# Gated cross-attention stack on one core: the first batch's loads come first, other preparation is queued behind its steps, and a sigmoid is written with tanh

## The chip, the core and the metric

The kernel runs on one core of one Trainium2 chip. The core has five engines that work side by side, each through its own queue in order: TensorE (PE: matmuls and transposes into PSUM banks), VectorE (DVE), ScalarE (ACT), GpSimd (POOL) and SyncE (SP, which here issues nearly all DMA loads and stores). The metric is the device time of one execution in microseconds (us), as the median of the runs shown.

## The reference

The input `x` has 8 batches of 256 tokens with 256 features, and the context `ctx_1024` the same shape. Four gated blocks follow one another:

```python
x = x + tanh(g_xattn[0]) * L0_xattn(layernorm(x), ctx)           # 16 heads of 16, keys and values from ctx
x = x + tanh(g_ffn[0])   * L0_slots(layernorm(x))                # routes to 64 slots, top 8, GRU update, gather back
x = x + tanh(g_xattn[1]) * L1_xattn(ctx, layernorm(x))           # 8 heads of 128 over 512 keys (ctx and x)
x = x + tanh(g_ffn[1])   * L1_ffn(layernorm(x), clip_x, clip_down)   # int8 fake-quantized gated FFN
```

The last block scales its activations by `sigmoid(clip) * max(abs(.)) / 127`, with one `clip` for its input and one for its hidden layer. The maximum of the input is taken over all batches, so that block starts when all the others are done.

## The kernel before

All tokens stay on the chip: `xs[b]` and `cs[b]` hold batch b of `x` and of the context, 128 partitions by 2 x 256. Layer 0 runs batch by batch. Batches 0 and 1 take a way of their own at the start; batches 2 to 7 are fed piece by piece into layer 1's loop from a queue (`side`). Layer 1's attention loops over 8 batches and 8 heads and takes most of the time; the FFN comes last.

**Tile framework.** The code records instructions; a scheduler then fixes the order of each engine's queue and inserts semaphore waits. So the order in the code is only a preference, unless there is a dependency. `tc.issue_after(ins)` puts what is recorded inside it behind `ins` where both are on the same engine. It adds no waiting on another engine.

**One batch of layer 0** (`Batch0`), in steps: `norm` (statistics and normalization on DVE, the power -1/2 on POOL: `ln_stats` L231, `ln_apply` L243), `turn_c` and `turn_x` (transposes on PE, copied out by ACT and DVE), `key` and `query` (projection L506 on PE, bias on ACT L528 and L520, then `split` L471, which splits the result into a high and a low part on DVE), `stack` (for batches 0 and 1 `spread` L550: small matmuls that place each head's rows into the operands `ks` and `qs`, copied out half by DVE L565 and half by ACT L566), `scores` (matmul L598, maximum on DVE L601), `maxima` (transposes L611, copied by ACT L612 into `qs`), `exps` (matmul L622, exponential on ACT L625), `sums`, `divide`, and at the end `turn_o` and `finish` (output projection L671 and residual add L678). Each batch has four groups of four heads. The operands carry eight more rows for the maxima; those of `ks` are filled once with the constant `pick` (DVE L192, four operands). Batch 0 uses the `m` banks of PSUM, batch 1 and later ones the `z` banks.

**Weights.** `wk` and `wq` exist in two layouts: as loaded (`wk_n`, `wq_n`, used by batches 0 and 1), and reordered by ACT (`by_place`, L174) for batches 2 to 7.

**Fill.** The slot block's weights must be transposed first: `fill` is a list of twelve pieces (`turn_slots`, `turn_w1`, `bias1`, three turns each for `wih` and `whh`, `gh`, `wv`, `wo`). A turn is four PE transposes (L254) into the one `s` bank and an ACT copy (L322). They are staged in memory that layer 1's weights take over later.

**The order at the start.** The SP queue issues the loads in code order: the context of batch 0, Wk, x of batch 0, Wq, two biases, Wv, bv, batch 1, Wo, then scalars, three bias rows broadcast to 128 partitions, the slot weights and the rest. Loads share eight semaphores in turn, so that each load waits for the one eight places before it. Constants are filled by POOL and DVE as they are allocated. Then batch 0 and batch 1 are interleaved by this loop:

```python
HEAD, LAG = 5, 10
for _, go in work0[0][:HEAD]:
    go()                          # norm, turn_c, key, turn_x, query of batch 0
second.pop(0)()                   # norm of batch 1
gates()
for n, go in enumerate(first):    # the rest of batch 0
    go()
    if n < len(fill):
        fill[n]()
    if n >= LAG:
        second.pop(0)()
by_place()
```

`gates` computes the tanh gates, the sigmoid of the two clips and the scalar `tau` on ACT, and scales three bias rows on POOL. After the loop come layer 1's loads, the first slot set (batch 0) and the rest of batch 1. Layer 1's first step, `media`, normalizes the context of batch 0.

Of the kernel before, what the change touches and what calls it, by code (L numbers as in the profile page):

```python
# [9 lines left out]
F32 = mybir.dt.float32  # L10
# [3 lines left out]
AF = mybir.ActivationFunctionType  # L14
ALU = mybir.AluOpType
# [4 lines left out]
P = 128  # L20
B, S, D = 8, 256, 256
EPS = 1e-5
H0, DK0 = 16, 16
HG = 4
NG = H0 // HG
NROW = 4 * DK0
# [63 lines left out]
def flamingo_kernel(ctx: ExitStack, tc: tile.TileContext, a: dict, out: bass.AP):  # L90
    nc = tc.nc
    V, A, G, T = nc.vector, nc.scalar, nc.gpsimd, nc.tensor
# [14 lines left out]
    x_in = a["x"].rearrange("b (t p) d -> b p t d", p=P)  # L107
    c_in = a["ctx_1024"].rearrange("b (t p) d -> b p t d", p=P)
    xs, cs = [], []
# [4 lines left out]
    def load_tokens(b, queue):  # L114
        queue.dma_start(out=xs[b], in_=x_in[b])
        queue.dma_start(out=cs[b], in_=c_in[b])
# [37 lines left out]
    wk, wq = (w0.tile([P, 2, D], F32, tag=n, name=n) for n in ("wk", "wq"))  # L154
    bk_n, bq_n = (pp_.tile([P, 2], F32, tag=n, name=n) for n in ("bkn", "bqn"))
    bk, bq = (w0.tile([P, 2], F32, tag=n, name=n) for n in ("bk", "bq"))
    nc.sync.dma_start(out=cs[0], in_=c_in[0])
    nc.sync.dma_start(out=wk_n, in_=a["L0_xattn_Wk"].rearrange("(c p) n -> p c n", p=P))
    nc.sync.dma_start(out=xs[0], in_=x_in[0])
    nc.sync.dma_start(out=wq_n, in_=a["L0_xattn_Wq"].rearrange("(c p) n -> p c n", p=P))  # L160
    for t, name in ((bk_n, "L0_xattn_bk"), (bq_n, "L0_xattn_bq")):
        nc.sync.dma_start(out=t, in_=a[name].rearrange("(c p) -> p c", p=P))
    wv = weight(w0, "wv", a["L0_xattn_Wv"], D)
    bv = rows(w0, "bv", a["L0_xattn_bv"], D, nc.sync)
    load_tokens(1, nc.sync)
    wo = weight(w0, "wo", a["L0_xattn_Wo"], D)

    def load_by_place():
# [5 lines left out]
    def by_place():  # L174
        for t, n in ((wk, wk_n), (wq, wq_n)):
            A.copy(t.rearrange("p c (e h) -> p c e h", e=DK0), n.rearrange("p c (h e) -> p c e h", e=DK0))
        G.tensor_scalar(bq4, bq, DK0**-0.5, None, ALU.mult)
# [5 lines left out]
    pick = w0.tile([2 * HG, HG], F32, tag="pick", name="pick")  # L183
    V.tensor_tensor(pick, ident[: 2 * HG, :HG], ident[: 2 * HG, HG : 2 * HG], ALU.add)

    def operand_pairs(pool, n):

        pairs = []
        for i in range(n):
            q = pool.tile([NROW + 2 * HG, HG, S], F32R, tag=f"qs{i}", name=f"qs{i}")  # L190
            k = pool.tile([NROW + 2 * HG, HG, S], F32R, tag=f"ks{i}", name=f"ks{i}")
            V.tensor_copy(k[NROW:, :, :], pick[:, :, None].to_broadcast([2 * HG, HG, S]))  # L192
            pairs.append((q, k))
        return pairs


    pairs_a, pairs_b = operand_pairs(pp_, 2), operand_pairs(w0, 2)

# [4 lines left out]
    for which, width, first, second in (("q", 160, 2, 3), ("k", 144, 1, 3)):  # L205
        t = pp_.tile([P, 4, width], F32R, tag=f"spread{which}", name=f"spread{which}")
# [6 lines left out]
    ident_b = keep.tile([P, P], BF16, tag="identb", name="ident_b")  # L213
    V.tensor_copy(ident_b, ident)
    ones = keep.tile([P, P], F32, tag="ones", name="ones")
    G.memset(ones, 1.0)
    mhalf = keep.tile([P, 2], F32, tag="mhalf", name="mhalf")
    G.memset(mhalf, -0.5)

# [22 lines left out]

    def ln_apply(dst, src, mv, scale):  # L243
        for i in range(2):
            V.tensor_scalar(
                dst[:, i, 0:D], src[:, i, :], mv[:, i, 0:1], scale[:, i : i + 1], ALU.subtract, ALU.mult
            )

    def transpose_pair(src, tag):

# [6 lines left out]
    def add_bias(b, row):  # L257
        return [G.tensor_tensor(xs[b][:, t, :], xs[b][:, t, :], row, ALU.add) for t in range(2)][-1]
# [14 lines left out]

    def gates():
        A.activation(gate, scal[:, 0:4], AF.Tanh)
        A.activation(clip, scal[:, 5:7], AF.Sigmoid)
        A.activation(tau, scal[:, 4:5], AF.Abs)
        V.tensor_scalar(tau, tau, 0.1, None, ALU.add)
        V.reciprocal(itau, tau)
        for row, g in ((gbo_a, g_x0), (gbo_f, g_f0), (gbo_b, g_x1)):  # L280
            G.tensor_scalar(row, row, g, None, ALU.mult)
# [148 lines left out]

    bq4 = w0.tile([P, 2], F32, tag="bq4", name="bq4")
    bq4_n = pp_.tile([P, 2], F32, tag="bq4n", name="bq4n")
    G.tensor_scalar(bq4_n, bq_n, DK0**-0.5, None, ALU.mult)

    def values_tile(pool):
        v = pool.tile([P, 2, H0, 2 * DK0], F32, tag="ve", name="ve")
        G.memset(v[:, :, :, DK0:], 1.0)
        return v

    places = {"a": (pp_, pairs_a, values_tile(pp_)), "b": (at0, pairs_b, values_tile(w0))}  # L440
    xn1 = w0.tile([P, 4, D + 1], F32, tag="xn1", name="xn1")
    G.memset(xn1[:, :, D : D + 1], 1.0)

    class Batch0:

# [25 lines left out]
        def split(self, name, full):  # L471

            hi, lo = self.halves(name)
            V.tensor_copy(hi, full)
            eng = V if self.b < 2 else G
            eng.tensor_tensor(lo, full, hi.bitcast(F32), ALU.subtract)
            if self.b < 2:
                return hi, lo
            name += self.s
            d = dram.tile([2, D, S], F32, tag=f"d{name}", name=f"d{name}")  # L480
            for i, x in enumerate((hi, lo)):
                nc.sync.dma_start(out=d[i].rearrange("(m p) t -> p m t", p=P), in_=x.bitcast(F32))
            return d.rearrange("i (e h) t -> i e h t", e=DK0)

        def norm(self):
            b = self.b
            self.xn = self.tmp(name="xn")
            mv, rstd = ln_stats(xs[b], "a" + self.s)
            ln_apply(self.xn, xs[b], mv, rstd)
            if b > 1:  # L490
                add_bias(b, gbo_a)

# [8 lines left out]
        def project(self, w, src):  # L501

            pp = self.bank().rearrange("p (m t) -> p m t", m=2)
            for m in range(2):
                for c in range(2):
                    T.matmul(  # L506
                        pp[:, m, :],
                        w[:, c, m * P : (m + 1) * P],
                        src[:, c, :],
                        start=c == 0,  # L510
                        stop=c == 1,
                    )
            return pp

        def query(self):
            w, bias = (wq_n, bq4_n) if self.b < 2 else (wq, bq4)
            pp = self.project(w, self.xnT)
            q = self.tmp(name="q")
            for m in range(2):
                A.activation(q[:, m, :], pp[:, m, :], AF.Identity, bias=bias[:, m : m + 1], scale=DK0**-0.5)  # L520
            self.dq = self.split("q", q)

        def key(self):
# [64 lines left out]
        def scores(self, g, qc):  # L588

            q, k = self.pairs[g % 2]  # L590
            if qc == 0:
                self.nm[g] = small.tile([P, 2, 2 * HG], F32R, tag=f"nm0{self.s}", name="nm0")
            full = small.tile([P, HG], F32, tag=f"nf0{self.s}", name="nf0")
            for half in range(2):
                ps = self.bank().rearrange("p (h k) -> p h k", h=2)
                for i in range(2):
                    j = 2 * half + i
                    T.matmul(  # L598
                        ps[:, i, :], q[:NROW, j, qc * P : (qc + 1) * P], k[:NROW, j, :], start=True, stop=True
                    )  # L600
                V.tensor_reduce(full[:, 2 * half : 2 * half + 2], ps, AX.X, ALU.max, negate=True)  # L601
            hi = self.nm[g][:, qc, :HG]
            V.tensor_copy(hi, full)
            V.tensor_tensor(self.nm[g][:, qc, HG:], full, hi.bitcast(F32), ALU.subtract)

        def maxima(self, g):

# [6 lines left out]
        def exps(self, g, half):  # L614

            q, k = self.pairs[g % 2]
            e = self.pool.tile([P, 2, 2, S], F32, tag="e", name="e", bufs=2)
            for i in range(2):
                j = 2 * half + i
                ps = self.bank().rearrange("p (c t) -> p c t", c=2)  # L620
                for kc in range(2):
                    T.matmul(  # L622
                        ps[:, kc, :], k[:, j, kc * P : (kc + 1) * P], q[:, j, :], start=True, stop=True
                    )
                A.activation(e[:, i, :, :], ps, AF.Exp)  # L625
            self.e[half] = e

        def sums(self, g):
# [309 lines left out]
    load_tokens(2, nc.sync)  # L938
    for c in range(2):
        nc.sync.dma_start(out=w1kv[:, c, :INNER], in_=a["L1_xattn_Wkv"][c * P : (c + 1) * P, :INNER])  # L940
    HEAD, LAG = 5, 10
    for _, go in work0[0][:HEAD]:
        go()
    first = [go for _, go in work0[0][HEAD:]]
    second = [go for _, go in work0[1]]
    second.pop(0)()
    gates()
    for b in range(2):
        add_bias(b, gbo_a)
    for n, go in enumerate(first):  # L950
        go()
        if n < len(fill):
            fill[n]()
        if n >= LAG:
            second.pop(0)()
    by_place()
    load_layer1()
    for _, go in slot_sets[0].pieces():
        go()
# [285 lines left out]
    def attention1():  # L1245
# [8 lines left out]
            return steps[n] if n < len(steps) else None  # L1254

        first = bs[0]
        first.media()
        first.latents()
        first.turn("m")
        first.turn("l")  # L1260
# [251 lines left out]
```

## Time and profile before

| | before |
|---|---|
| median of 3 runs | 1047.76 us (1046.73 to 1048.28) |
| profiled execution | 1043.28 us |
| its span in the profile | 1041.5 us |
| busy: PE, DVE, ACT, POOL | 990.5, 623.7, 463.9, 121.5 us |
| mean granted clock of PE | 0.975 |

The span runs from the first to the last instruction in the trace; 1.8 us of the execution lie around it. The granted clock is the share of PE's full clock that the chip's throttle let through, by stretch. Matmuls are pipelined and their ends are modelled, so a PE that is shown busy can still be slow or partly waiting. In the prediction's lines, the timeline gives start and length in us, engine, line, operation, output and input tiles, and in brackets the idle time of the engine before it with what ended it.

### The profile page before, as it was taken

To read this page: it belongs to the slowest core of one execution; us is meant where nothing else is said; L and a number is where in the kernel's file an instruction comes from. 1 tells how busy PE (TensorE), PEld (TensorE's weight loads), DVE (VectorE), ACT (ScalarE), POOL (GpSimd) and SP (SyncE) were. 2 spreads that over 40 slices of the span, in tenths; PEclk is the share of its full clock that TensorE was granted. 3 is DMA by queue.
4 is the path that set the end of the run, shared out by engine and by line. 5 is a ranking of instruction groups with operands and counts; after the bars stand their busy time and mean duration, and the time that the engine had idled before them with its cause. 6 is when DMAs were issued, how large, how long until landed. Compare 5 with 4: busy or idle time off the path is not lost.

```text
span 1041.5 us, 13065 instructions
## 1 busy us (share of the span) xinstructions
PE 990.5 (95%) x4803; PEld 683.5 (66%) x4803; DVE 623.7 (60%) x1613; ACT 463.9 (45%) x878; POOL 121.5 (12%) x158
## 2 busy tenths in 40 slices
PE   5998799999999999999999999999999999999776
PEld 4765466667677667777776676676776776776423
DVE  5655566656465655756566564566765365454397
ACT  3666335444435533444534434444334234234474
POOL 5201120101010010111001000010000000000134
PEclk9989889999999999999999999999999999999897
DMA  7702200021110101111000100001000000000002
GB/s 172 200 1 72 91 21 21 28 74 41 52 50 22 51 31 41 36 46 41 21 21 31 51 21 21 29 1 56 1 1 1 1 0 1 1 1 1 1 0 82
DMA packets 33536, 37.32 MB, mean 36 GB/s; under 512 B 10368, under 2 KB 28992, under 8 KB 33472
## 3 DMA queue, kind: packets, MB, share of 16 engines
q1 hardware_dynamic: 33472, 36.48, 11.9%
q8 instruction: 38, 0.62, 0.2%
q14 instruction: 26, 0.21, 0.1%
HBM read 28.08 MB, written 8.39 MB: 35 GB/s over the span
## 4 chain that ended last, share of the span: by engine, by line
PE 87%; DVE 7%; ACT 2%; DMA 2%; issue 1%; POOL 1%; SPq 0%; DVEq 0%; ACTq 0%; POOLq 0%
PE bank_m L1020 11%; PE bank_m L1051 11%; PE bank_m L1079 10%; PE bank_m L1033 10%; PE bank_m L1005 6%; PE bank_m L1065 5%; PE bank_m L1092 5%; PE bank_z L598 4%; PE bank_z L635 3%; PE bank_z L622 3%; PE bank_z L506 2%; PE bank_z L535 1%; PE bank_s L845 1%; PE bank_z L671 1%; PE bank_m L254 1%; PE bank_m L635 1%
## 5 line engine op out<-in xcount | busy, mean ns | idle before, releaser
L1053 ACT ACTIVATE e<-bank_m,nm 128x512 f32<-128x512 f32 x128 | 88.0, 688 | 146.2 <-DVE nm L1052 144.0
L1051 PE MATMUL bank_m<-k,q 128*128 128x512 f32 x256 | 127.3, 602 | 0.0
L1020 PE MATMUL bank_m<-kvT,w1kv 128*128 128x512 f32 x256 | 126.1, 604 | 0.0
L1079 PE MATMUL bank_m<-eT,v 128*128 128x256 f32 x512 | 124.8, 381 | 1.1 <-ACT e L1053 0.7
L1079 PEld LDWEIGHTS bank_m<-eT,v 128*128 128x128 f32 x512 | 95.3, 190 | 34.4 <-issue 16.3
L1033 PE MATMUL bank_m<-w1kv,kvT 128*128 128x256 f32 x512 | 116.6, 380 | 0.0
L1052 DVE TENSOR_REDUCE nm<-bank_m 128x1 f32<-128x512 f32 x128 | 87.9, 688 | 33.7 <-PE bank_m L1051 32.9
L1033 PEld LDWEIGHTS bank_m<-w1kv,kvT 128*128 128x128 f32 x512 | 95.9, 190 | 13.7 <-issue 1.1
L625 ACT ACTIVATE e<-bank_z 128x512 f32<-128x512 f32 x112 | 63.2, 596 | 80.9 <-PE bank_z L622 80.7
L240 POOL TENSOR_TENSOR rstd<-rstd,mhalf 128x2 f32<-128x2 f32 x48 | 34.7, 726 | 446.6 <-DVE rstd L239 410.1
L1014 DVE TENSOR_SCALAR q<-bank_m,bq 128x256 f32<-128x256 f32 x64 | 28.1, 479 | 97.1 <-PE bank_m L1005 97.0
L601 DVE TENSOR_REDUCE nf<-bank_z 128x2 f32<-128x512 f32 x112 | 75.0, 683 | 18.0 <-PE bank_z L598 17.6
L1040 DVE COPY v<-bank_m 128x512 f32<-128x512 f32 x64 | 43.9, 686 | 58.0 <-PE bank_m L1033 58.0
L1065 PEld LDWEIGHTS bank_m<-ident,e 128*128 128x128 f32 x512 | 58.5, 140 | 23.4 <-issue 18.2
L1065 PE MATMUL bank_m<-ident,e 128*128 128x128 f32 x512 | 71.4, 275 | 0.4 <-DVE v L1040 0.4
L1022 ACT ACTIVATE k<-bank_m,bk 128x512 f32<-128x512 f32 x64 | 44.0, 688 | 55.2 <-PE bank_m L1020 55.1
L1086 ACT ACTIVATE oT<-bank_m,bv 128x256 f32<-128x256 f32 x64 | 30.3, 474 | 84.4 <-PE bank_m L1079 84.1
L1005 PE MATMUL bank_m<-kvT,w1q 128*128 128x256 f32 x256 | 64.1, 388 | 1.3 <-DVE kvT L991 1.0
L1055 DVE TENSOR_SCALAR e<-e,rs 128x512 f32<-128x512 f32 x128 | 62.1, 485 | 2.2
L1051 PEld LDWEIGHTS bank_m<-k,q 128*128 128x128 f32 x256 | 44.5, 190 | 26.6 <-issue 22.0
L1020 PEld LDWEIGHTS bank_m<-kvT,w1kv 128*128 128x128 f32 x256 | 43.0, 190 | 28.1 <-issue 24.6
L1092 PE MATMUL bank_m<-w1o,oT 128*128 128x256 f32 x256 | 59.6, 380 | 0.6 <-DVE x L1106 0.6
(345 smaller groups left out, 1547.8 us busy)
## 6 DMA issues: line engine op xcount, KB each, us to landing
qs<-dqb SPq DMA_DIRECT2D x96, 64.0 KB, 2.5
ks<-dkb SPq DMA_DIRECT2D x48, 128.0 KB, 2.7
c<-in_ctx_dram SPq DMA_DIRECT2D x8, 256.0 KB, 3.2
x<-in_x_dram SPq DMA_DIRECT2D x8, 256.0 KB, 2.9
w1kv<-in_L_xattn_Wkv_dram SPq DMA_DIRECT2D x4, 512.0 KB, 6.8
out_dram<-y SPq DMA_DIRECT2D x8, 256.0 KB, 2.1
dqb<-hi SPq DMA_DIRECT2D x6, 256.0 KB, 2.1
dqb<-lo SPq DMA_DIRECT2D x6, 256.0 KB, 2.4
```

What stands on the lines that cost most here:

```text
L601: V.tensor_reduce(full[:, 2 * half : 2 * half + 2], ps, AX.X, ALU.max, negate=True)
L625: A.activation(e[:, i, :, :], ps, AF.Exp)
L1005: T.matmul(pq[:, i, :], w1q[:, c, h * P : (h + 1) * P], self.kvT[:, c, S:], start=c == 0, stop=c == 1,)
L1020: T.matmul(pk, w1kv[:, c, h * P : (h + 1) * P], self.kvT[:, c, :], start=c == 0, stop=c == 1)
L1033: T.matmul(pv[:, k, :], self.kvT[:, c, kc * P : (kc + 1) * P], w1kv[:, c, at : at + 2 * P], start=c == 0, stop=c == 1,)
L1051: T.matmul(ps, self.q[h][:, qc * P : (qc + 1) * P], self.k[h], start=True, stop=True)
L1052: V.tensor_reduce(nm[:, at], ps, AX.X, ALU.max, negate=True)
L1053: A.activation(e[:, qc, :], ps, AF.Exp, bias=nm[:, at], accum_out=sums[:, at])
L1055: V.tensor_scalar(e[:, qc, :], e[:, qc, :], rs[:, at], None, ALU.mult)
L1065: T.transpose(pt[:, k, qc * P : (qc + 1) * P], self.e[h][:, qc, kc * P : (kc + 1) * P], ident)
L1079: T.matmul(po, self.v[h // 2][:, kc, (h % 2) * P : (h % 2 + 1) * P], self.eT[:, kc, :], start=kc == 0, stop=kc == 3,)
L1092: T.matmul(self.pp[:, qc, :], self.oT[:, h, qc * P : (qc + 1) * P], w1o[:, h, :], start=h == 0, stop=h == H1 - 1,)
```

## The change

Five things change together.

1. **Loads.** SP issues x and the context of batch 0, then Wk, Wq, then batch 1, then Wv, bv and Wo. The two biases are issued by ACT's queue.
2. **Constants.** The fills of the maxima rows of the second batch's two `ks` operands (`rows_for_maxima(pairs_b)`), of `ve`, `ones` and `xn1`, and the scaling of the query bias, stand behind steps of the first batch: POOL's behind its first power, DVE's behind the key split of batch 0.
3. **Sigmoid.** `sigmoid(c)` becomes `0.5 * tanh(0.5 * c) + 0.5`: the ACT function is Tanh, as for the gates, and DVE does one more small operation. `gates` stands behind batch 0's query bias on ACT.
4. **Second batch and fill.** The pieces of batch 1 start two places earlier in the loop (LAG 8), but behind batch 0's query projection on PE and its query split on DVE. The fill starts seven places later (FILL).
5. **Reordered weights and layer 1.** `by_place` moves into the loop, behind the first exponentials of batch 0 on ACT. Layer 1's first `media` stands behind the last maxima of batch 0 on DVE.

```diff
-    nc.sync.dma_start(out=cs[0], in_=c_in[0])
+    load_tokens(0, nc.sync)
     nc.sync.dma_start(out=wk_n, in_=a["L0_xattn_Wk"].rearrange("(c p) n -> p c n", p=P))
-    nc.sync.dma_start(out=xs[0], in_=x_in[0])
     nc.sync.dma_start(out=wq_n, in_=a["L0_xattn_Wq"].rearrange("(c p) n -> p c n", p=P))
     for t, name in ((bk_n, "L0_xattn_bk"), (bq_n, "L0_xattn_bq")):
-        nc.sync.dma_start(out=t, in_=a[name].rearrange("(c p) -> p c", p=P))
+        nc.scalar.dma_start(out=t, in_=a[name].rearrange("(c p) -> p c", p=P))
+    load_tokens(1, nc.sync)
     wv = weight(w0, "wv", a["L0_xattn_Wv"], D)
     bv = rows(w0, "bv", a["L0_xattn_bv"], D, nc.sync)
-    load_tokens(1, nc.sync)
...
-            V.tensor_copy(k[NROW:, :, :], pick[:, :, None].to_broadcast([2 * HG, HG, S]))
...
+    def rows_for_maxima(pairs):
+        for _, k in pairs:
+            V.tensor_copy(k[NROW:, :, :], pick[:, :, None].to_broadcast([2 * HG, HG, S]))
+
+    rows_for_maxima(pairs_a)
...
-        A.activation(clip, scal[:, 5:7], AF.Sigmoid)
+        A.activation(clip, scal[:, 5:7], AF.Tanh, scale=0.5)
         A.activation(tau, scal[:, 4:5], AF.Abs)
+        V.tensor_scalar(clip, clip, 0.5, 0.5, ALU.mult, ALU.add)
...
+    def fill_constants():
+        G.tensor_scalar(bq4_n, bq_n, DK0**-0.5, None, ALU.mult)
+        for _, _, v in places.values():
+            G.memset(v[:, :, :, DK0:], 1.0)
+        G.memset(ones, 1.0)
+        G.memset(xn1[:, :, D : D + 1], 1.0)
...
-    HEAD, LAG = 5, 10
-    for _, go in work0[0][:HEAD]:
-        go()
-    first = [go for _, go in work0[0][HEAD:]]
-    second = [go for _, go in work0[1]]
-    second.pop(0)()
-    gates()
+    def after(*instructions):
+        stack = ExitStack()
+        for ins in instructions:
+            stack.enter_context(tc.issue_after(ins))
+        return stack
+
+    b0 = batches0[0]
+    first, second = ([go for _, go in work0[b]] for b in range(2))
+    first.pop(0)()
+    with after(b0.normed, powers[0]):
+        fill_constants()
+    HEAD, LAG, FILL = 4, 8, 7
+    for _ in range(HEAD):
+        first.pop(0)()
+    with after(b0.split_ins):
+        rows_for_maxima(pairs_b)
+        second.pop(0)()
+    with after(b0.bias_ins):
+        gates()
     for b in range(2):
         add_bias(b, gbo_a)
+    query_ins, split_ins = b0.project_ins, b0.split_ins
     for n, go in enumerate(first):
         go()
-        if n < len(fill):
-            fill[n]()
+        if n >= FILL and n - FILL < len(fill):
+            with after(query_ins):
+                fill[n - FILL]()
         if n >= LAG:
-            second.pop(0)()
-    by_place()
+            with after(query_ins, split_ins):
+                second.pop(0)()
+        if n == LAG:
+            with after(b0.exp_ins):
+                by_place()
...
-        first.media()
+        with tc.issue_after(batches0[0].max_ins):
+            first.media()
```

`normed`, `split_ins`, `project_ins`, `bias_ins`, `max_ins` and `exp_ins` are new names for the last instruction of the step in question. Lines of the changed kernel are some 10 to 30 higher: L613 is the score reduction (L601 before), L822 the first transpose of the routing weights in the slot block (L810 before).

## The prediction

> **What bounds the kernel now.** Three views, from coarse to fine: the slices of the page, busy time by stretch, and the timeline and waits of the first 30 us. The times are those of the one profiled execution.
>
> ```profile
> PE   5998799999999999999999999999999999999776
> PEclk9989889999999999999999999999999999999897
> DMA  7702200021110101111000100001000000000002
> ```
>
> TensorE (PE) is full from the second slice (26 us each) to the last three. A gain must remove PE idle time or time at a slow clock; it lies in the first four slices. In the next view, by stretch, the first pair of numbers is the stretch and its length, PEclk the granted clock.
>
> ```profile
> 0.00:10.00 10.00, 1.09 (x4) 0.72 (x4) 4.73 (x15) 3.87 (x4) 6.10 (x24) 1.00 0.67 192
> 10.00:20.00 10.00, 6.37 (x21) 5.20 (x22) 6.98 (x22) 3.11 (x7) 6.69 (x8) 0.88 0.77 115
> 60.00:65.00 5.00, 4.61 (x26) 3.15 (x24) 3.22 (x9) 4.67 (x9) 0.00 (x0) 1.00 0.00 0
> 65.00:70.00 5.00, 5.00 (x18) 2.49 (x18) 3.26 (x9) 1.31 (x3) 0.00 (x0) 0.54 0.00 0
> 70.00:75.00 5.00, 5.00 (x37) 3.42 (x36) 1.19 (x7) 1.83 (x2) 0.00 (x0) 0.77 0.00 0
> 90.00:95.00 5.00, 3.50 (x33) 2.33 (x25) 2.93 (x11) 4.07 (x8) 3.31 (x4) 1.00 0.49 125
> ```
>
> PE idles 12.5 us in the first 20, then almost nothing until 60. A hold at 60 to 62.6 is followed by a stretch at 0.54 and 0.77 of the clock, worth 5 x 0.46 + 5 x 0.23 = 3.45 us. At 90 to 95 it idles 1.5 us. The timeline shows what the first batch waits for (start, length, idle before it):
>
> ```profile
> 7.54 0.28 POOL L433 TENSOR_SCALAR bq4n<-bqn 128x2 f32<-128x2 f32 x1 [3.33 <-DMA bqn<-in_L_xattn_bq_dram]
> 7.74 3.30 DVE L192 CAST ks<-pick 8x1024 fp32r<-8x1024 f32 x4
> 9.30 2.28 POOL L240 TENSOR_TENSOR rstd<-rstd,mhalf 128x2 f32<-128x2 f32 x2
> 11.07 0.74 DVE L245 TENSOR_SCALAR x<-x,mv,rstd 128x256 f32<-128x256 f32 x2
> 11.37 0.69 PE L254 MATMUL bank_z<-ident,c 128*128 128x128 f32 x2 [6.65 <-DMA c<-in_ctx_dram]
> 15.82 1.28 ACT L276 ACT_TABLE_LOAD   x1
> 18.86 2.99 PE L506 MATMUL bank_m<-c,c 128*128 128x256 f32 x8
> 19.62 0.82 DVE L346 TENSOR_SCALAR slots<-slots,sscale 128x256 f32<-128x256 f32 x1 [1.60 <-DMA sscale<-in_L_ffn_slot_scale_dram]
> 27.13 1.29 DVE L601 TENSOR_REDUCE nf<-bank_m 128x2 f32<-128x512 f32 x2 [0.27 <-PE bank_m L598]
> ```
>
> The first batch's rstd waits behind a bias load and fills on POOL, its normalization behind four fills on VectorE (DVE). Its key projection waits behind the second batch's transposes on PE, its query projection (18.86) behind the second batch's key projection, whose input waits for the table load on ScalarE (ACT). The slots row matters most below.
>
> **Loads, POOL and ACT at the start.** With x0, c0, Wk, Wq first in the SP queue, the four land as the first four did: used at 3.52, 4.27, 6.36 and 7.09. The two bias loads go to the ACT queue beside them; their own landing took 4.2 to 4.5 us, so x0 lies between 3.5 and 4.5. I take 3.5: it decides nothing. The statistics end at 4.7, POOL's power takes 0.7, two fills instead of four 1.65, so x0 is normalized near 7 and not 11.8. ACT loses both weight copies here (2 x 1.05). The key projection runs from 6.4, as Wk lands, to 9.5; transposes and copy add 1.2; the query projection takes 10.7 to 13.7 (3.0 as in its row) instead of 18.86 to 21.85. So far the first batch leads by 8 us.
>
> **Where that lead goes.** In the built order, the slots multiply stands on DVE right behind the first batch's key split, ahead of the first ks copy and of the query split. It waits for four loads on SP, each of which also waits for the load eight places earlier. The same bytes stand ahead of them, the three 128 KB bias rows among them; while these run, 13 to 17 us, the DMA view gives only 41 to 72 GB/s. So it still starts near 19.6: at earliest 18.0, where DVE began to wait for it; at latest 20.9, by the spread of the four loads' landing times (5.2 to 6.5 us). DVE stands still from about 12 on, PE from about 14.
>
> From 19.6 DVE runs, in its built order: slots 0.7 (row: 0.82), ks copy 0.65, query split 0.35 + 0.6, clip and tau 0.2, two moved fills 1.65, second batch's statistics 0.75 + 0.35, three copies 3 x 0.65, its normalization 0.75: about 8.0. The first score reduction starts at 27.6, against 27.13. Four reductions at 0.65 and small operations (0.85) end at 31.05, as before (31.06).
>
> Now the fills of wih have left this place. Before, their transposes and copies stood between the two maxima transposes, and ACT's copy of the maxima ran at 32.39; then a second table load (34.02, 1.28) ran ahead of the first exponential at 35.31. The change has neither: sigmoid by tanh leaves one set for tanh and exp. Maxima copy 31.3 to 32.3, score transposes for the exponentials at 32.3 instead of 33.92, first exponential at 32.65. The lead is 1.6 us on PE. But PE has then not done three wih turns (3 x 0.45) and one query half (0.43): 1.8. Net: **+0.2**.
>
> A rule weighed here. The Trainium skill, "ScalarE: Activation LUTs", section "What ACT_TABLE_LOAD costs", gives about 1.28 us for the load and 1.38 us more of drain per switch. The trace shows 1.28, with the previous ACT operation ending at 15.80 and the next starting at 17.11: no drain. By the page the saved load would be worth 2.66, and the sum 1.4 lower.
>
> **The middle, 35 to 60.** The eight remaining weight turns (0.59 each on ACT) and the two reordering copies (2.1) move to where ACT also copies the second batch's eight spread halves (8 x 0.58). ACT has no gap from 49.4 to 62.6 before; I put this stretch at about 41 to 54. Exponentials hold PSUM banks there while PE has little else: laying PE's rows against ACT's gives PE about 1.9 us of waiting, against 0.3 before: **+1.6**, between 0 (fills cover it) and 3.7 (all of the 2.1 on top).
>
> **The hold at 60 and the slow clock.** The second batch's spreads are then through earlier, and first-batch exponentials no longer queue behind them at 60. If the hold goes (0.57 idle in 60 to 80) and the slow stretch with it (3.45): **-4.0**; bounds -4.0 and 0, because nothing says that a hold cannot form elsewhere. I take -4.0: the rows at 60 name ACT's queue as the cause, and the change empties it 8 us sooner.
>
> A rule speaks against this. The Trainium skill, "TensorE: Matmul & The Clock Gate", Part 1, says that PE falls to half clock after an idle window of about 3.4 us. This trace has 0.54 after a shorter hold. By the page the changed kernel's idle time from 14 to 20 makes another half-speed window after it, some 1.7 us if PE were the limit there.
>
> **The join.** From the first L810 (103.89) on, both kernels queue the same PE work in the same order. Just ahead of it, the finish of the first batch (L671) moves behind the third batch's whole query projection. Before, that query's split (ACT 0.85, DVE 0.43, POOL 1.28) stood in front of POOL's power: 3.46 us from the last matmul at 89.64 to the normalization at 93.10. After it is through before; residual add 0.7, statistics 0.95, rstd 0.1, power 0.7, about 2.5: **-0.9**, in a stretch where PE idles; bounds -1.5 and 0.
>
> Moved at no cost: the statistics of the context (about 3 us of DVE) go to about 75 to 90, where DVE is busy under half; without that cover, 1 us or so. POOL's fills follow the first power at about 5.5, its gates stay near 15, and POOL has nothing else due there. SP's later loads keep their order, except that small layer-1 loads pass the w1kv and w1q halves, which wait longer for the turns; their first reader comes at 138.
>
> **Sum.** +0.2 + 1.6 - 4.0 - 0.9 = -3.1. The execution's own time is 1043.28 (span 1041.5), so it would be 1040.2. The timed median is 4.5 above the profiled one, 1047.76; I carry the difference: 1044.7.
>
> **Rivals.** (1) *Handed back*: the hold only moves, to 47 to 54, and the slow stretch follows it. Then -4.0 falls to about -1: near 1047.7. For it: the rows show half clock after each hold (30 to 35 has 0.66). Against: fewer copies stand in ACT's queue by then. (2) *Slower*: DVE's queue behind the slots loads. For it: DVE has 8 us to run after the landing, nothing else shortens that, and it waited for the same loads before. A landing at 20.9 adds 1.3; with the hold staying: 1.3 + 0.2 + 1.6, the join gain lost, gives +3.1, 1050.9. It decides from a landing after about 20.4, where half the 1.6 lead is gone, or a first reduction after 28.5. Against it: the same bytes stand ahead of them. (3) *The change doesn't do what it says*: the first batch is first only up to its key split; that is in the sum.
>
> **Numbers.** A difference of 0.2% (2.1 us) is about what a measurement here can tell from none. My case 0.44, handed back 0.22, slower 0.34. The range 1041 to 1051.5 runs from my case with the middle at 0 and a landing 1.6 earlier (-6.3), up to the slower one with 0.6 of the 2.1 by which the middle's upper bound lies above what I took. My case alone: 1041.5 to 1046.0, the upper end with a landing 1.3 later.
>
> **What would show it.** Slots multiply at 18 to 21 on DVE with some 8 us idle before it; query projection near 11; first L613 reduction near 27.6; one table load before the Gelu; no stretch near 0.5 between 55 and 80; first L822 near 101. Wrong: slots at 15, or PE held and slow between 45 and 75.

## The result, and the profile after

The change makes no difference that can be measured. Its median is 1046.68 us (12 runs, 1044.46 to 1048.06) beside 1045.76 us for the kernel before (12 runs); the ratio is 1.001, with a 95% interval of 0.9996 to 1.0023. A second series gave 1045.96 against 1045.74 us, 0.9998 (0.9981 to 1.0014). The forecast was 1044.7 us in the range 1041 to 1051.5, with "faster" as the likeliest case (0.44; 1041.5 to 1046.0). The range holds the time, but that case did not come: what came is the rival "handed back", which had a chance of 0.22.

One slip in the text above: VectorE's fills stand behind batch 0's query split, not its key split (item 2 of the change).

The profiled execution took 1048.06 us (span 1046.2, granted clock 0.967). First the slices of its page, to be held against those of before:

```profile
PE   5899889999999999999999999999999999999776
PEclk9798889999999999999999999999999999999897
DMA  7512200021020101011000100001000000000002
```

The clock is lower in the second slice (7) and later back at 9. By stretch (length, then busy time of PE, PE's weight load, DVE, ACT and POOL, then the granted clock):

```profile
15.00:20.00 5.00, 0.85 (x3) 0.47 (x3) 1.85 (x4) 0.59 (x4) 4.17 (x5) 0.90 0.55 129
20.00:25.00 5.00, 5.00 (x28) 4.77 (x28) 4.71 (x16) 2.82 (x6) 0.72 (x1) 0.76 0.94 308
25.00:30.00 5.00, 3.06 (x15) 1.65 (x13) 4.66 (x11) 2.11 (x4) 2.55 (x3) 0.93 0.89 274
30.00:35.00 5.00, 4.37 (x15) 3.47 (x15) 2.60 (x9) 2.08 (x3) 0.45 (x2) 0.50 0.93 268
35.00:40.00 5.00, 5.00 (x17) 4.19 (x17) 3.21 (x10) 3.11 (x4) 0.00 (x0) 0.50 0.11 34
50.00:55.00 5.00, 4.50 (x27) 3.28 (x26) 4.08 (x11) 4.89 (x10) 0.00 (x0) 1.00 0.30 110
55.00:60.00 5.00, 4.88 (x17) 2.19 (x17) 1.65 (x7) 1.71 (x4) 0.00 (x0) 0.66 0.35 108
60.00:65.00 5.00, 5.00 (x32) 3.11 (x31) 1.80 (x3) 3.23 (x5) 0.00 (x0) 1.00 0.00 0
65.00:70.00 5.00, 5.00 (x32) 4.21 (x31) 3.83 (x11) 4.33 (x9) 0.00 (x0) 1.00 0.00 0
80.00:85.00 5.00, 5.00 (x21) 2.62 (x19) 2.52 (x10) 2.92 (x6) 1.38 (x2) 0.55 0.00 0
```

The hold at 60 is gone, as forecast: from 60 to 70 PE is full at full clock. But two other holds stand ahead of it, each with half clock behind. PE idles 1.94 us in 25 to 30, and 30 to 40 runs at 0.50. It idles 0.50 us in 50 to 55, where ACT is busy 4.89 of 5 us, and 55 to 60 runs at 0.66. The timeline of the start shows why PE waits:

```profile
6.97 3.78 PE L516 MATMUL bank_m<-cT,x 128*128 128x256 f32 x8 [0.68 <-ACT cT L505]
12.38 1.99 PE L516 MATMUL bank_m<-c,c 128*128 128x256 f32 x8 [0.78 <-DVE c L509]
18.15 0.94 DVE L352 TENSOR_SCALAR slots<-slots,sscale 128x256 f32<-128x256 f32 x1 [4.76 <-DMA sscale<-in_L_ffn_slot_scale_dram]
19.01 0.67 DVE L577 CAST ks<-bank_m 64x512 fp32r<-64x512 f32 x1
25.86 1.93 DVE L613 TENSOR_REDUCE nf<-bank_m 128x2 f32<-128x512 f32 x3
28.97 1.28 POOL L389 TENSOR_TENSOR gh<-gh,w1q 128x512 f32<-128x512 f32 x1 [2.35 <-DMA gh<-in_L_ffn_gru_bhh_dram]
29.04 1.23 DVE L615 CAST nm<-nf 128x4 fp32r<-128x4 f32 x1
31.00 1.00 ACT L624 CAST qs<-bank_m 8x1024 fp32r<-8x1024 f32 x1 [3.39 <-PE bank_m L623]
33.54 1.08 ACT L637 ACTIVATE e<-bank_m 128x512 f32<-128x512 f32 x2 [1.55 <-PE bank_m L634]
```

The query projection runs at 12.4 instead of 18.9. Then DVE stands 4.76 us at the slots multiply, the first ks copy comes at 19.0, the maxima are copied at 31.0 and the first exponential runs at 33.54, against 35.31 in the profile of before (33.80 in its second one).

**Where all differences lie.** From the first PE transposes of `al` on (L810 before, L822 after), every profile of this study needs another 937.2 to 938.6 us to the end (only those of experiments 5 and 6 need 939.6 and 940.3). So what counts is when that point comes, and what is lost ahead of it. The table adds half-microsecond stretches of the windows view: idle is length less PE's busy time, slow-clock cost is busy time times (1 - granted clock). The second and third profiles come from the runs below.

| profile | point at | PE idle | slow-clock cost | the rest |
|---|---|---|---|---|
| before | 103.89 | 17.4 | 6.6 | 79.9 |
| before, second | 106.01 | 15.8 | 10.2 | 80.0 |
| after | 108.93 | 16.2 | 14.6 | 78.1 |
| after, second | 105.98 | 15.8 | 12.5 | 77.7 |
| after, third | 103.33 | 16.6 | 9.0 | 77.7 |

The same program comes to that point 2 to 6 us earlier or later, and the slow clock makes most of the scatter. Without it the point lies at 97.3 and 95.8 before, and at 94.3, 93.5 and 94.3 after: 2.5 us earlier on average. The slow clock costs 8.4 before and 12.0 after: 3.6 more. These are means of two and of three profiles that differ by as much among themselves; the timed runs below carry the comparison.

### The profile page after: what moved, and what is told of

The parts are those of the page before. It is cut to its first block, busy times and chain, and to the rows that moved or that the text cites. A ratio compares the mean times of both kernels' runs of the same rounds, so it can differ in the third digit from the quotient of the medians.

```text
span 1046.2 us, 13068 instructions
## 1 busy us (share of the span) xinstructions
PE 996.6 (95%) x4803; PEld 687.1 (66%) x4803; DVE 623.3 (60%) x1614; ACT 460.6 (44%) x876; POOL 119.3 (11%) x158
## 4 chain that ended last, share of the span: by engine, by line
PE 86%; DVE 7%; ACT 3%; DMA 1%; issue 1%; POOL 1%; SPq 0%; ACTq 0%; DVEq 0%; POOLq 0%
PE bank_m L1081 11%; PE bank_m L1050 11%; PE bank_m L1109 10%; PE bank_m L1063 10%; PE bank_m L1035 6%; PE bank_m L1095 5%; PE bank_m L1122 5%; PE bank_z L610 4%; PE bank_z L647 3%; PE bank_z L516 3%; PE bank_z L634 3%; PE bank_z L547 1%; PE bank_s L857 1%; PE bank_m L258 1%; PE bank_z L683 1%; PE bank_z L258 1%
## 5 line engine op out<-in xcount | busy, mean ns | idle before, releaser
L613 DVE TENSOR_REDUCE nf<-bank_z 128x2 f32<-128x512 f32 x112 | 74.9, 683 | 15.8 <-PE bank_z L610 15.5
L1116 ACT ACTIVATE oT<-bank_m,bv 128x256 f32<-128x256 f32 x64 | 30.3, 473 | 84.1 <-PE bank_m L1109 83.8
```

## Experiments

**How runs are compared.** Each timed run has its span and mean granted clock. I call span times (1 - clock) the run's clock loss. Over the runs of all kernels, each kernel taken about its own mean, the span grows by 0.74 us for each us of clock loss (correlation 0.91). The last column puts each kernel's spans on that line at a loss of 30.3 us, plus or minus its standard error. It is a fit and no experiment: half clock that falls on idle time costs nothing, but counts in the loss, and the slopes of the single kernels lie between 0.56 and 1.00 (before 0.76, after 0.57). The errors given leave this out.

| kernel | median us | ratio to before (95%) | median clock | mean clock loss | span at equal loss |
|---|---|---|---|---|---|
| before (87 runs) | 1044.7, 1044.9, 1045.7 in three series | 1 | 0.974 | 28.5 | 1045.2 ± 0.1 |
| after (24 runs) | 1046.68, 1045.96 | 1.001, 0.9998 | 0.967 | 33.3 | 1042.0 ± 0.2 |
| tanh alone | 1046.74 | 1.0016 (0.9997 to 1.0034) | 0.970 | 32.2 | 1044.1 ± 0.2 |
| slots late | 1047.45 | 1.0016 (0.9999 to 1.0033) | 0.966 | 35.4 | 1041.0 ± 0.4 |
| slots late, 3 extra matmuls | 1044.03 | 0.9981 (0.9962 to 0.9999) | 0.971 | 29.5 | 1042.1 ± 0.3 |
| extra matmuls, first try | 1047.51 | 1.0025 (1.0009 to 1.004) | 0.973 | 29.4 | 1046.2 ± 0.3 |
| extra matmuls, second try | 1049.45 | 1.0034 (1.0017 to 1.0052) | 0.969 | 31.4 | 1046.3 ± 0.3 |
| all late (17 runs) | 1042.50, 1040.26 | 0.9963 (0.9944 to 0.9981), 0.9944 (0.9922 to 0.9966) | 0.971 | 30.3 | 1039.3 ± 0.1 |
| all late, 2 extra matmuls | 1044.07 | 0.998 (0.996 to 1.0) | 0.971 | 31.4 | 1041.6 ± 0.3 |
| all late, loads of before | 1044.21 | 0.9978 (0.996 to 0.9995) | 0.9675 | 33.3 | 1040.0 ± 0.3 |

**1 and 2. Both kernels unchanged, a second profile.**

> The kernel before, unchanged, for a second profile. Theory A (the slow clock belongs to the stall ahead of it): the hold of TensorE at 60 to 62.6 us and the half clock right behind it (0.54 at 65 to 70) are there again, within 1 us of the same place, and so are the short ones at 18 to 21 and 31 to 35; the span is within 1.5 us of 1041.5. Theory B (the slow clock has a pattern of its own, which a stall only helps along): the hold at 60 is there again, since the instructions and their order are the same, but the half-clock stretches of the first 104 us differ in number or length by over 3 us in all, and the first L810 moves from 103.9 by over 1.5 us.

> The changed kernel, unchanged, for a second profile. Theory A: the half clock from 29 to 42 us, at 56 to 60, 80 to 87 and 104 to 107 is there again, the first L822 within 1 us of 108.9 and the span within 1.5 us of 1046.2. Theory B: the stalls (14 to 19, 28 to 31, the finish at 91) are at the same places, but the half-clock stretches are not; the first L822 lies 2 us or more earlier than 108.9, because the medians of the two kernels differ by 0.9 us and their profiled executions by 4.8.

Second profile of before, stretches as above:

```profile
60.00:65.00 5.00, 4.91 (x19) 3.78 (x19) 3.14 (x8) 3.34 (x8) 0.00 (x0) 0.57 0.00 0
65.00:70.00 5.00, 5.00 (x15) 2.53 (x16) 2.45 (x8) 0.59 (x2) 0.00 (x0) 0.50 0.00 0
95.00:100.00 5.00, 5.00 (x16) 3.50 (x15) 2.09 (x6) 3.72 (x5) 0.00 (x0) 0.50 0.41 143
```

Neither theory holds alone. Slow stretches belong to places: behind the hold near 60 in both profiles of before, and at 30 to 40 and 55 to 60 in all three of after. Their number and length are not fixed: the half clock at 18 and 31 of the first profile of before is missing in the second, which has ten us of it from 95 on instead. The common point came 2.1 us later in the second profile of before and 3.0 us earlier in that of after, as theory B had it. Of the changed kernel's stretches, the one at 80 to 87 is in the first profile only.

**3. The slots' work behind the first reductions (slots late).**

```diff
+        if n == 3:
+            mx = b0.max_ins
...
-            with after(query_ins):
+            with after(query_ins, mx):
                 fill[n - FILL]()
```

> VectorE's multiply of the slots, with the rest of the first weight-turn steps, stands behind the first score reductions instead of ahead of the first ks copy. Queue theory (VectorE's queue behind the slots' loads costs the whole lead): the first ks copy runs at about 13.5 instead of 19.0, the first L613 reduction at 20 to 22 instead of 25.9, the first exponential at 27 to 30 instead of 33.5, TensorE idles 3 to 4 us less before 31, and the time is 2 to 4 us lower than the changed kernel's, about 1043 to 1044.5. Clock theory (what the start gains goes back at half clock): the same times in the trace up to 30, but the half clock behind 29 stays or moves, the first L822 comes less than 1.5 us earlier than before's L810, and the time is within 1 us of 1046.

```profile
14.11 0.68 DVE L577 CAST ks<-bank_m 64x512 fp32r<-64x512 f32 x1 [1.50 <-PE bank_m L569]
22.30 1.87 DVE L613 TENSOR_REDUCE nf<-bank_m 128x2 f32<-128x512 f32 x3
25.91 0.34 DVE L352 TENSOR_SCALAR slots<-slots,sscale 128x256 f32<-128x256 f32 x1
```

The first ks copy comes at 14.1 instead of 19.0, the first reduction at 22.3, the first exponential at 30.56; PE idles 11.4 us before the score matmuls of the exponentials, against 13.3 to 14.1. Both theories had that, though each of the three times came 0.3 to 0.6 us later than expected, and the gain in idle time is 2 to 3 us and not 3 to 4. The time is 1047.45 all the same, above what either theory gave, at the lowest clock of all kernels. At equal loss it is 1.0 us ahead of the changed kernel, and its clock loss is 2.1 us larger, which at 0.74 costs 1.6. That is nearer the clock theory.

**4. The same with three extra matmuls where PE waits for the maxima.**

```diff
+            if self.b == 0 and g == 0:                    # in maxima(), ahead of the transposes
+                self.extra(3, self.score_ins, pt)         # T.matmul(pt, ident, wq_n), 128 x 512, pt is overwritten
```

> The kernel with the slots' work behind the first score reductions, plus three extra matmuls on TensorE between the first batch's last score matmul and the transposes of its maxima (23.5 to 26.4), where it had stood still for 1.5 us. No work is left out. Clock theory: the median granted clock rises from 0.966 to 0.970 or more, and the time falls by 2 to 4 us from 1047.45, to 1043.5 to 1045.5. Rival: the half-clock windows come whatever is done there, the clock stays at 0.966, the time at 1047 to 1048.

The stretch 25 to 30 without and with them:

```profile
25.00:30.00 5.00, 4.40 (x12) 2.92 (x13) 2.98 (x9) 1.49 (x3) 1.26 (x1) 0.50 1.03 342
```

```profile
25.00:30.00 5.00, 5.00 (x15) 2.47 (x14) 2.49 (x9) 0.82 (x1) 1.26 (x1) 0.76 0.99 334
```

More work, and 3.4 us less time. (The two were timed in different series; before had 1044.7 and 1044.9 us in them.) At equal loss the kernel is 1.1 us slower (± 0.5), which would be the price of the extra matmuls. The clock loss falls by 5.9 us, which at 0.74 is worth 4.4. Apart from the three, PE's queue holds the same instructions in the same order to the end. So in this place filling the stall with useless work kept the clock up, and that was worth more than the work cost.

**5 and 6. Extra matmuls in the changed kernel's two stalls.** First try with `xs[0]` as operand, four and three; second with `wq_n`, five and two.

> Seven extra matmuls (128 x 512, written into banks that are overwritten at once) are put into the two stretches in which TensorE of the changed kernel stands still: four between the first batch's key spread and its query spread (14.5 to 19), three between its last score matmul and the transposes of its maxima (28 to 31). No work is left out. Clock theory: the half clock from 29.4 to 42 goes, the stretch 30 to 45 is granted 0.9 or more, the first L822 comes 3 to 5 us earlier than 108.9, and the time is 1 to 4 us lower than the changed kernel's although it does more. Rival (the idle time there is not what sets the clock off): the half clock comes at about the same place and length, the extra matmuls cost what they displace, 0 to 3 us.

> As the run before with extra matmuls, but they read the query weights, which nothing rewrites, instead of the first batch's input, which POOL updates and for which they had waited until 20.5 us. Five extra matmuls behind the first batch's key spread (about 4.8 us from 14.6, at 0.95 us each), two behind its last score matmul. No work is left out. Clock theory: with TensorE busy from 14.6 to 19.4 and from 28 to 30, the median granted clock of the timed runs rises from the changed kernel's 0.967 to 0.971 or more, and the time falls by 1 to 3 us, to 1043.5 to 1045.5. Rival (the extra work only displaces other work): the clock rises or not, the time stays at 1046 to 1048.

In the first try they waited for POOL, which updates x of batch 0, and so delayed the queries instead of filling the gap:

```profile
20.51 6.04 PE L566 MATMUL bank_m<-x,ident 128*128 128x512 f32 x8 [5.34 <-POOL x L262]
```

In the second they ran at 14.67 as meant, but the scheduler put the second batch's key projection behind the maxima (35.3 instead of 23.5), and the first exponential came at 38.2. Both kernels' clock loss falls, by 3.9 and 1.9 us, and both are 4.2 to 4.3 us slower at equal loss. For the changed kernel's own stalls the time thus settles nothing. The profiles go with the clock theory, one each. In the first try PE is full from 25 to 40 us, where the changed kernel has its second stall, and the half clock from 29 to 42 is gone, as that theory expected:

```profile
25.00:30.00 5.00, 5.00 (x27) 3.42 (x25) 2.70 (x5) 1.66 (x4) 2.50 (x3) 0.97 0.97 308
30.00:35.00 5.00, 5.00 (x23) 2.95 (x21) 3.23 (x12) 2.10 (x5) 0.51 (x2) 1.00 0.89 277
35.00:40.00 5.00, 5.00 (x30) 4.26 (x30) 2.88 (x10) 4.23 (x7) 0.00 (x0) 1.00 0.37 27
```

In the second PE is idle for 2.4 us between 19.5 and 25 instead, and half clock runs from 21.4 to 35.0.

**7. Tanh alone, in the kernel before.**

```diff
-        A.activation(clip, scal[:, 5:7], AF.Sigmoid)
+        A.activation(clip, scal[:, 5:7], AF.Tanh, scale=0.5)
         A.activation(tau, scal[:, 4:5], AF.Abs)
+        V.tensor_scalar(clip, clip, 0.5, 0.5, ALU.mult, ALU.add)
```

> The kernel before with one part of the change alone: the clip's sigmoid as 0.5 + 0.5 tanh(x/2). One table load (1.28 us) ahead of the first exponential goes, and the scheduler moves what it likes. Theory that table loads on the path cost their length: first exponential at about 34.0 instead of 35.3, the time 0.5 to 1.5 us lower than before's, about 1043.5. Rival (TensorE has other work there and the clock decides): the time within 0.7 us of before's, the scatter of the runs following the granted clock, by 0.5 to 0.8 us for each us that the clock loses.

ACT's timeline, then two stretches:

```profile
30.92 0.58 ACT L323 COPY wihT<-bank_s 128x512 f32<-128x512 f32 x1
31.49 1.08 ACT L626 ACTIVATE e<-bank_m 128x512 f32<-128x512 f32 x2
```

```profile
55.00:60.00 5.00, 4.56 (x27) 2.77 (x22) 2.35 (x7) 4.10 (x6) 0.00 (x0) 0.98 0.00 2
60.00:65.00 5.00, 4.99 (x18) 3.99 (x17) 2.90 (x7) 2.93 (x7) 0.00 (x0) 0.50 0.00 0
```

The first exponential runs at 31.49, right behind a copy, with no table load in between; before it was at 35.31 and 33.80. Two table loads are gone and not one: that at 15.82 (16.23 in the second profile) ahead of the sigmoid, and that at 34.02 (32.50) ahead of the exponential; of the loads ahead of 90 us only the one at 0.74 is left. At equal loss all this is worth 1.1 us, less than the two loads' 2.56; the scheduler also moved score reductions and query splits on VectorE, so the part of the loads alone isn't known. The hold near 60 and the slow stretch behind it stay, the clock loss grows by 3.7 us (2.7 at 0.74), and the kernel is not faster.

**8 and 9. VectorE does only the first batch until its maxima are there (all late).** On top of number 3, the second pair's fills and the second batch's normalization:

```diff
-    with after(b0.split_ins):
-        rows_for_maxima(pairs_b)
-        second.pop(0)()
...
         if n == 3:
             mx = b0.max_ins
+            with after(mx):
+                rows_for_maxima(pairs_b)
+                second.pop(0)()
```

> The kernel with the slots' work behind the first score reductions, and behind them also VectorE's fills for the second pair of operands and the second batch's normalization: VectorE does nothing but the first batch until its maxima are there. Queue theory: the first L613 reduction at 19 to 20 us instead of 22.3, the first exponential at 25 to 27 instead of 29.6 (TensorE), and at a granted clock of 0.971 the span is 1 us lower than that kernel's 1040.5 to 1042.9. Clock theory: the same times in the trace, but the median granted clock is 0.967 or lower, as in the other kernels that start the first batch early, and the median time is within 1.5 us of 1046.5. A granted clock of 0.972 or more with a median under 1044 would say that the first batch's early start and a high clock do go together.

> The kernel in which VectorE does nothing but the first batch until its maxima are there, a second time. If its gain is one of the order of the work, it repeats: 1 to 4 us below before's median, at equal granted clock 5 to 6 us below; the clock near 0.969. If it was a chance of that hour on the chip, the median comes back to within 1 us of before's.

Timeline of the second run:

```profile
16.81 0.68 DVE L577 CAST ks<-bank_m 64x512 fp32r<-64x512 f32 x1 [3.29 <-PE bank_m L569]
21.46 1.89 DVE L613 TENSOR_REDUCE nf<-bank_m 128x2 f32<-128x512 f32 x3 [0.49 <-PE bank_m L610]
26.38 1.09 ACT L637 ACTIVATE e<-bank_m 128x512 f32<-128x512 f32 x2 [0.59 <-PE bank_m L634]
26.52 0.32 DVE L352 TENSOR_SCALAR slots<-slots,sscale 128x256 f32<-128x256 f32 x1
```

This version is faster than the kernel before, by 0.37% and 0.56% in its two series; in the second it is also 5.7 us faster than the changed kernel (1040.26 against 1045.96). The first exponential comes at 24.48 and 26.38 in its two profiles, 7 to 10 us earlier than in the changed kernel, and PE idles 9.9 us ahead of the score matmuls instead of 13.3 to 14.1. At equal loss that is 2.7 us ahead of the changed kernel. And the clock loss is 30.3, not 33.3: an early start and a fair clock go together here, though the median clocks of the two series, 0.969 and 0.9715, stay short of the 0.972 that the expectation had set as the mark. Why they do in this order and not in number 3's, the runs don't show.

**10. The same with two extra matmuls ahead of the maxima.**

> That kernel with two extra matmuls (1.9 us at full clock) between the first batch's last score matmul and the transposes of its maxima, where TensorE had some 2 us of waiting. No work is left out. Clock theory: the half-clock windows that begin at 25 us go or shrink, the median granted clock rises from 0.969 to 0.972 or more, the time falls by another 1 to 2 us to about 1041. Rival: the extra matmuls delay the maxima by 0.5 to 1 us and the clock stays; 1042.5 to 1043.5.

Nearer the rival, and worse than it: no gain in clock loss (31.4 against 30.3), 2.3 us slower at equal loss, and 1044.07 us where the rival had at most 1043.5. In its profile the slow window at 25 is gone, but PE is busy only 0.69 of the 3 us from 29 to 32, and half clock follows there. Filling a stall doesn't always pay.

**11. The same with the loads of before.**

> That kernel with the loads of before: context, key weights, input, query weights, biases on SP, the second batch's tokens behind the value weights. If the loads carry the gain at the start, the first batch's statistics run at 6.4 instead of 4.1 us, its query projection and first reduction come 2 to 2.5 us later than in the kernel it is made from, and the time is 1.5 to 2.5 us higher. If the order on VectorE carries it, the loads are worth under 1 us, as TensorE has the key projection and the second batch's transposes to do meanwhile.

```profile
6.21 0.75 DVE L240 BATCH_NORM_STATS2 st<-x 128x6 f32<-128x256 f32 x2 [6.21 <-DMA x<-in_x_dram]
18.66 1.89 DVE L614 TENSOR_REDUCE nf<-bank_m 128x2 f32<-128x512 f32 x3 [0.49 <-PE bank_m L611]
```

x arrives 2.1 us later than with the new loads (4.15 and 4.19), and the first reduction is still no later (18.66 against 19.49 and 21.46). So the early first reduction is one of VectorE's order and not of the loads. For the time the runs are less clear. The median is 1044.21, 4.0 us above the same kernel with the new loads in the same series (1040.26) and 1.7 above its first series (1042.50): as timed, the 1.5 to 2.5 us that were expected of loads that carry the gain were met or passed. The clock loss is 3.0 us larger (33.3 against 30.3), worth 2.2 at 0.74, and at equal loss 0.7 us is left (± 0.3). That the loads are worth only 0.7 holds at equal clock loss; why the clock is lower with the old loads, the runs don't show.

**12. The changed kernel timed once more.**

> The changed kernel, unchanged, timed beside the kernel before and the three others of this series. Two-term theory (the change gains at the start, and the clock takes it back): its median granted clock is again lower than before's (0.967 against 0.974), and at equal clock (0.971) its span is 1.5 to 3 us shorter than before's; the medians differ by 0 to 2 us, this one slower. Rival (the change gains nothing at all): at equal clock the spans agree within 0.7 us.

The two-term theory holds: clock 0.9675 against 0.972, medians 0.2 us apart, and at a clock of 0.971 the median span is 1042.6 us (5 runs of both series) against 1045.5 (18 runs of before). Its third profile has the same two holds and slow stretches as the first, but not the one at 80:

```profile
35.00:40.00 5.00, 5.00 (x19) 4.06 (x19) 3.22 (x9) 3.39 (x5) 0.00 (x0) 0.50 0.18 60
50.00:55.00 5.00, 4.50 (x26) 3.23 (x26) 4.67 (x13) 4.90 (x10) 0.00 (x0) 0.97 0.28 107
55.00:60.00 5.00, 5.00 (x18) 2.07 (x16) 1.05 (x6) 1.23 (x3) 0.00 (x0) 0.69 0.37 108
80.00:85.00 5.00, 5.00 (x29) 2.40 (x28) 2.40 (x7) 2.31 (x6) 0.95 (x2) 1.00 0.00 0
```

## Why the prediction was right or wrong

**The net, in one line.** At equal clock loss the change is worth -3.2 us (± 0.5 by the scatter of the runs); its clock loss grows from 28.5 to 33.3, which at 0.74 is +3.5. By the changed kernel's own slope of 0.57 it would be -2.4 and +2.7. Either way the two nearly cancel, as the runs of number 12 had been expected to show. The forecast of -3.1 looks like the first number by chance: its largest term was made of clock.

**Start, +0.2: the number right, in part by errors that cancel.** PE's idle time ahead of the exponentials' score matmuls is 13.9 and 13.2 us before, 13.5, 13.3 and 14.1 after. The mechanism held: VectorE's queue stood at the slots and took the lead back. Slots waited until 18.15 (17.95 and 18.67 in the other profiles), at the early bound of 18.0 and 1.5 earlier than taken. DVE stood still for 4.8 us, not 8: the wait ended 1.5 early, and it began later, since PE's key projection began 0.6 us late and took 3.78 us and not 3.1 (it ran at half clock throughout; see the last section). The reductions began at 25.9 to 26.7, earlier than 27.6, but the maxima were copied at 30.9 to 31.7 (forecast 31.3): in two of three profiles a small cast took 1.23 us beside POOL's `gh`. The score matmuls follow at 32.5, 32.5 and 33.2 (forecast 32.3). What was weak is the lead of 1.6 us: it was read off a single profile of before, with its score matmuls at 33.92; the second has them at 31.93, ahead of all three of after.

**Middle, +1.6: oversized, measured 0.** From there to the first batch's finish PE idles 0.9 us in both profiles of before, and 0.8 to 0.9 after. The two reordering copies run at 37.19 to 39.21 and ACT then waits 2.88 us for its next work: they were covered. The busy stretch of ACT came, but at 46.8 to 56.7 and not at 41 to 54.

**Hold and slow clock, -4.0: the step that failed.** The hold at 60 did go. But ACT's full queue held PE in 50 to 55, and half clock followed between 55 and 60, in all three profiles. The one wait of PE that the timeline lists between 49 and 60 us is for ACT's copy of a `qs` half, here in the first profile (in the others at 52.87 and 53.12, as long):

```profile
53.71 0.50 PE L610 MATMUL bank_z<-ks,qs 64*128 64x256 f32 x2 [0.27 <-ACT qs L578]
```

That is the rival "handed back" with its mechanism and nearly its place (47 to 54). It had priced this at a remaining -1. It was worse: behind the stall at 25 to 31 there are also three to four slow windows of 3.41 us, in all three profiles, where the first profile of before has one (at 31) and the second none. The slow-clock cost ahead of the common point went from 6.6 and 10.2 to 14.6, 12.5 and 9.0: +3.6 on average instead of -3.45, and the mean clock loss of the timed runs rose by 4.8 us. The mistake was to book a slow stretch to the one hold ahead of it and to strike both out, while nothing in the sum stood for the two stalls that the forecast itself drew: PE still from 14 to 19, for which it named a window of some 1.7 us but left it out, and the wait at the maxima. That these stalls set off the half clock is argued from its place in three profiles and from the profiles of numbers 4 and 5, where it goes as the stall is filled; against it stands number 10. What these stalls cost the changed kernel isn't shown, as numbers 5 and 6 delayed other work.

**The rule that was weighed.** The Trainium skill, "TensorE: Matmul & The Clock Gate", Part 1, has half clock after an idle window of about 3.4 us. By it the prediction noted a further slow window after 14 to 20. It came in all three profiles (20 to 25 at 0.76, 0.59 and 0.60), so the page spoke rightly against the change; the first profile of before has one there too (17.7 to 21.1), the second none. It doesn't cover the rest: 50 to 55 has 0.50 us of idle in all and a slow stretch behind it. The same section says that the window runs freely and that a kernel's count of slow matmuls varies between runs. The slow-clock cost of the two profiles of before varies too (6.6 and 10.2 us).

**Join, -0.9: oversized.** Between the finish and the common point PE idles 2.6 and 1.7 us before, and 1.8 in each of after: -0.4.

**Not in the sum.** The rest in the first table (neither idle nor slow) fell from 80 to 77.7 to 78.1 us for the same matmuls (477 of them in the traces of before, 481 in those of after). It isn't the half clock at the very start that the records don't show (last section): an estimate of its cost, half of PE's busy time up to the first recorded change of clock, is 2.0 and 3.1 us before and 2.9, 2.3 and 2.2 after, the same on average. What the 2 us are stays open. About 1.1 us of the gain at equal loss may be the tanh, by experiment 7, which removes two table loads; the forecast priced only the second, inside the lead of 1.6.

**The rival "slower": its mechanism is real, its sign was not.** VectorE's queue does hold the first batch back: taking the slots, the fills and the second batch's normalization out of its way is worth 2.7 us at equal loss. But in the kernel before the queue waits for the slots too (1.60 us in the prediction's row), and at equal loss the changed kernel is ahead of it, so the change doesn't lose by it.

**The base.** The median of 1047.76 came from three runs. The later series have 1044.7 to 1045.8, so carrying 4.5 us from the profiled execution to the median was 2 to 3 us too much. That covered for half of the error in the sum: the change was +0.9 us instead of -3.1, the time only 2.0 above the forecast.

What removes the hold at 60 was not tried apart; tanh alone doesn't. Of the five parts of the change only the tanh was tried alone, and the loads only within the version of number 8, so which part brings the larger clock loss isn't known either.

## What to carry to other kernels

Where a program sits near a throttle, read two numbers for each run, the time and the granted clock, and compare kernels at equal clock: 2.5 to 3.2 us gained and 3.5 to 3.6 lost again look like a change that does nothing. A single profile can't price a stall here, as the same program differs by 3.6 to 5.6 us in slow-clock cost from one execution to the next. If one batch is to go first, look at every engine's queue and not only at the loads: at equal clock loss the new loads were worth 0.7 us, VectorE's order 2.7.

## What the runs showed of the hardware

- The half clock comes in whole windows: 3.41 us or two to four times that in all profiles, but for the one that the program's end cuts off, with a grid that lies differently against the program in each execution.
- It doesn't take a long stall: 0.5 us of idle time within 5 us was followed by 3.4 us of half clock in three profiles of three. Yet in the first profile of before 1.5 us of idle in 90 to 95 was followed by none, and in the second 1.7 us in the same place by 10.2 us. The rule behind it stays open.
- The clock row isn't reliable at the very start. It shows 1.00 up to 15 us of the changed kernel's profile, but there eight 128 x 256 matmuls took 3.78 us (at 6.97), and eight of the same shape 1.99 us (at 12.38). A single one lasts 634 ns or more among the first and 379 ns among the second. Matmuls of that shape last 634 ns in the kernel before too, from 11.8 to 14 us, where the row shows 1.00, and again from 18.9 to 20.6, where it shows 0.50. So the first matmuls run at half clock, and the row doesn't show it.
- A 128 x 4 cast on DVE took 1.23 us instead of 0.16 where it began 0.07 and 0.08 us after a POOL operation of 1.28 us on two SBUF operands; where it began after that operation's end (30.13 in the second profile), 0.16. In all three profiles the VectorE operation that was caught ended 0.02 to 0.03 us after POOL's; in the second it was the subtraction ahead of the cast, 0.59 us instead of 0.15.
